# A convolution, attention and expert kernel: the last part in one periodic list, and reciprocal roots moved from POOL to ACT

## The chip, the cores and the metric

The kernel runs on one core of a Trainium2 chip. The core's engines work side by side: TensorE (PE, matmuls; its weight loads are told apart as PEld), VectorE (DVE), ScalarE (ACT), GpSimd (POOL) and SyncE (SP, which here issues transfers). The metric is the time of one execution on the device, in microseconds. The tensors are float32 throughout.

## The reference

The input `x` is 32 images of 128 channels of 64 x 64 pixels. Cut to what matters:

```python
# layer 0: group norm, then a convolution in a learned transform domain, and a residual
x_f = tensor_product(gn(x), k11, k12)             # 64x64 complex matrices along h and w
w_f = tensor_product(weight, kd1, kd2) * 64
prod = einsum('bihw,oihw->bohw', x_f, w_f)         # mixes the 128 channels at each frequency
x = x + real(tensor_product(prod, k21, k22))
# layer 1: tokens are pixels, t is (32, 4096, 128)
n = ln(t)                                         # mean and variance over 128 channels, eps 1e-5
k, v = n @ Wk.T + bk, n @ Wv.T + bv
probs = softmax(einsum('sbe,sbf->sef', k, v) / sqrt(32))   # a 128x128 matrix for each image s
t = t + einsum('sef,sbf->sbe', probs, n)
n = ln(t)
gate = top 2 of softmax(n @ router_w + router_b) over 8 experts, renormalised
t = t + sum over the two chosen experts of gate * (n @ expert_w + expert_b)
```

In the attention the kernel works image by image: for one image it needs the 128 x 128 matrix of products summed over that image's 4096 tokens. Both `ln` steps divide by sqrt(variance + eps), a value for each token.

## The kernel before

The kernel has three parts. The first normalises the images and transforms them into frequencies; the second mixes channels; both are untouched. The last part, from line 788 on, does everything else: the inverse transforms, the residual, attention and experts. It loops over the 32 images, and each image passes through four steps, whose functions are nested in the kernel:

- `transfers(b)`: SP loads eight row tiles `r0` to `r7` (512 KB each, in two transfers) and the image itself, `x` (2 MB, tile `y` in the profile).
- `conv(b)`: for each row tile PE makes the inverse along w, `w0` to `w7` (tile `pu`, L903, into the single PSUM buffer `cv`), and ACT writes it out in two halves, `wo` (L913). Four inverses along h follow, `h0` to `h3` (tile `py`, L925), and DVE adds each to the image, `ho` (L933). The first two images use smaller pieces in the experts' PSUM buffers (L946, L965).
- `front(b)`: PE turns the image into tokens, four token tiles at a time, `pt` (L1049), ACT copies them out, `to` (L1054), DVE takes statistics, `sa` (L1021). DVE makes variances, `va` (L1031 to L1036); POOL raises them to the power -1/2, `pwa` (L1041); DVE makes the shifts, `na` (L1078). ACT normalises, `xg` (L1089), PE sums products, `pg` (L1100). A short chain over the 128 x 128 matrix follows: `gs`, `pb`, `t1`, `pb2`, `sm`, `pr`, `sr`, `sn`, `pc`, `prx`. Then eleven groups of PE products `pp` (L1173), ACT scaling `at` (L1186), DVE addition with statistics `ad` (L1201). The second norm follows: `vb`, `pwb` (again L1041), router logits `lg`, `nb`, `l2`, and the choice of two experts, `f1` to `f5` and `gt` (L1246 to L1276).
- `experts(b)`: ACT normalises, `xn` (L1301), PE turns back, `px` (L1311), ACT copies, `xT` (L1317). For each of 32 token tiles PE makes two halves of expert products, `pe0_0` to `pe31_1` (L1324), and DVE multiplies each by the gates, `m` (L1335). POOL sums the products of two token tiles, `s0` to `s15` (L1360 to L1363). PE turns the result, `st` (tile `po`, L1370), ACT copies it, `so` (L1376), SP stores it (L1377). For the last image five of the sixteen sums are made on DVE instead (L1347).

Buffers: three PSUM tiles for expert products (`pe`), three for everything else of small size (`tl`), two product tiles `tm` between DVE and POOL, two each of `xn`, `xT`, `so`.

Each step is an operation in a plan with its engine, an assumed duration, a due time, what it comes after, and counted buffers that it takes and frees. Due times are the image's number plus an offset, plus a shift for its kind (`SHIFT`), in slots of 114 us. `Plan.run` plays the plan with the assumed durations; at each free engine it starts the earliest due operation that is ready and has its buffers. The order so found is the order of the program: each engine carries out its own instructions in that order and waits where the next one is not ready. The store's transfer is issued in the same operation as ACT's copy `so`.

The table of the power's exponents, `mhalf`, holds -0.5 in 32 columns; variances lie as 128 x 32.

Of the kernel before, what the change touches and what calls it, by code (L numbers as in the profile page):

```python
# [10 lines left out]
F32 = mybir.dt.float32  # L11
# [5 lines left out]
P = 128  # L17
# [7 lines left out]
class Plan:  # L25
# [12 lines left out]
    def run(self):  # L38
# [46 lines left out]
        self.length = now  # L85
        for i in order:
            ops[i][3]()
# [3 lines left out]
def kernel(  # L91
# [737 lines left out]
    def prepare():  # L829
# [23 lines left out]
    plan = Plan({"cv": 1, "pe": 3, "tl": 3, "r": 10, "x": 2, "xg": NG, "xn": 2, "xT": 2, "tm": 2, "so": 2, "gate": 2})  # L853
    SLOT = 114.0

    SHIFT = {
        "ad": -0.15, "at": -0.25, "f": 0.71, "gs": -1.97, "gt": 0.71, "h": -0.24, "ho": -3.5, "kvp": 3.43,
        "kvq": -0.45, "l": 0.71, "lg": 3.61, "m": -0.32, "na": -1.87, "nb": -0.81, "pb": -1.97, "pc": -1.97,
        "pe": 0.16, "pg": -0.08, "pp": 0.19, "pr": -1.97, "prx": -1.97, "pt": -0.23, "pwa": -1.87, "pwb": 3.61,
        "px": 0.15, "r": -0.04, "s": 0.08, "sa": 1.29, "sm": -1.97, "sn": -1.97, "so": 2.13, "sr": -1.97,  # L860
        "st": 1.1, "t": -1.97, "to": 0.06, "va": -1.87, "vb": 3.61, "w": 0.28, "x": -0.68, "xT": -0.68,
        "xg": 0.21, "xn": 2.42,
    }
    made = {}

    def add(b, key, engine, us, at, run, after=(), take=(), free=(), late=0.0):


        names = [k if isinstance(k, tuple) else (b, k) for k in after]
        at += SHIFT.get(key.rstrip("0123456789_"), 0.0)  # L870
        made[b, key] = plan.add(
            engine, us, SLOT * at, run, [made[k] for k in names if k[0] >= 0], take, free, late
        )


    def transfers(b):
# [4 lines left out]
        def load_r(e):  # L881
            def run():
                i = 8 * b + e
                ring, tag = (rp, "r") if i % 10 < 8 else (rp2, "r2")
# [10 lines left out]
        add(b, "x", "SP", 0.1, b + 0.2, load_x if b else (lambda: None), take=("x",), late=12.0 if b else 0.0)  # L895

    def conv(b):
        def w_inverse(e):

            def run():  # L900
                ps = tile_of["cv", b, e] = cps.tile([P, 8, P], F32, tag="cv", name=f"pu{b}_{e}")
                for k in range(8):
# [3 lines left out]
                    )  # L906
            return run
# [31 lines left out]
        def w_inverse_piece(e, oh):  # L939

            def run():
                ps = tile_of["cw", b, e, oh] = eps.tile([P, 8, n], F32, tag="pe", name=f"pw{b}_{e}_{oh}")
                for k in range(8):
                    lo = (2 * k + oh) * n
                    for r in range(2):
                        nc.tensor.matmul(  # L946
                            ps[r * n : (r + 1) * n, k, :], rs[b, e][:, lo : lo + n], qw[:, r, :], start=True, stop=True
                        )
            return run
# [28 lines left out]
        if b < 2:  # L978
            for e in range(8):
                at = b + 0.08 * e  # L980
                for oh in range(2):
                    add(
                        b, f"w{e}_{oh}", "PE", 0.95, at + 0.04 * oh, w_inverse_piece(e, oh),
                        [f"r{e}"] + [(b - 1, f"h{k}") for k in range(4)], ("pe",), ("r",) if oh else (),
# [13 lines left out]
            if b == 0:  # L998
                add(b, "prep", "PE", 3.5, 0.98, prepare, ["h3"], ("pe",), ("pe",))
# [14 lines left out]
    def front(b):  # L1014
# [24 lines left out]
        def power(which):  # L1039
            total, var, nmr, rstd = v[which]  # L1040
            nc.gpsimd.tensor_tensor(rstd, var, mhalf, ALU.pow)  # L1041
# [26 lines left out]
        for g in range(8):  # L1068
# [3 lines left out]
            add(b, f"sa{g}", "DVE", 0.85, at, stats1(g), [f"to{g}"] + (["sa0"] if g else []))  # L1072
        add(b, "va", "DVE", 1.7, s1 + 0.14, lambda: moments(1), [f"sa{g}" for g in range(8)])
        add(b, "pwa", "POOL", 5.5, s1 + 0.14, lambda: power(1), ["va"])

        def nmr1():
            total, var, nmr, rstd = v[1]
# [3 lines left out]
        add(b, "na", "DVE", 0.9, s1 + 0.14, nmr1, ["pwa"])  # L1081
# [74 lines left out]
        add(b, "pb", "PE", 0.35, at, kv1, ["gs"], ("tl",))  # L1156
# [48 lines left out]
        for j, lo in enumerate(range(0, NT, 3)):  # L1205
            m = min(3, NT - lo)
            at = s1 + 0.45 + 0.016 * j
            add(b, f"pp{lo}", "PE", 0.26 * m, at, product(lo, m), ["prx", (b - 1, "lg")], ("tl",), ("x",) if lo == 30 else ())
# [29 lines left out]
        def nmr2():  # L1238
            total, var, nmr, rstd = v[2]
# [41 lines left out]
        add(b, "pwb", "POOL", 5.5, at, lambda: power(2), ["vb"])  # L1281
        add(b, "lg", "DVE", 1.95, at, logits1, ["vb"])
        add(b, "nb", "DVE", 2.1, at + 0.1, nmr2, ["pwb", "lg"])
        add(b, "l2", "DVE", 1.95, at + 0.1, logits2, ["nb"], ("gate",))
# [7 lines left out]
    def experts(b):  # L1292
# [79 lines left out]

        def store(g):
            def run():
                so = wp.tile([P, 512], F32, tag="so", name=f"so{b}_{g}")
                nc.scalar.copy(so, tile_of.pop(("po", b, g)))  # L1376
# [92 lines left out]
```

## Time and profile before

| | |
|---|---|
| median of 3 runs | 6039.6 us (6039.03 to 6046.36) |
| the profiled execution | 6034.45 us, its span 6032.7 us |
| busy PE, PEld, DVE, ACT, POOL | 5884.8, 4672.1, 4220.6, 3757.1, 4205.9 us |
| last part | 2536.5 us to the end |
| granted PE clock, mean | 0.994 |

A line of a profile names the engine, the line of the kernel, and the tiles written and read (`out<-in`). Busy time is the union of an engine's instructions. "Idle before" is the time in which the engine did nothing just before the instruction, with the one that ended it behind `<-`. The chain of waits is followed back from the last instruction, at each step to what released it. PE instructions are pipelined, so that one begins before the last has ended: what a piece costs PE is read from the starts of two that follow each other.

### The profile page before, as it was taken

To read this page: it belongs to the slowest core of one execution; us is meant where nothing else is said; L and a number is where in the kernel's file an instruction comes from. 1 tells how busy PE (TensorE), PEld (TensorE's weight loads), DVE (VectorE), ACT (ScalarE), POOL (GpSimd) and SP (SyncE) were. 2 spreads that over 40 slices of the span, in tenths; PEclk is the share of its full clock that TensorE was granted. 3 is DMA by queue.
4 is the path that set the end of the run, shared out by engine and by line. 5 is a ranking of instruction groups with operands and counts; after the bars stand their busy time and mean duration, and the time that the engine had idled before them with its cause. 6 is when DMAs were issued, how large, how long until landed. Compare 5 with 4: busy or idle time off the path is not lost.

```text
span 6032.7 us, 219314 instructions
## 1 busy us (share of the span) xinstructions
PE 5884.8 (98%) x95372; PEld 4672.1 (77%) x95372; DVE 4220.6 (70%) x7696; ACT 3757.1 (62%) x7057; POOL 4205.9 (70%) x3793
## 2 busy tenths in 40 slices
PE   7999999999999999989999999999999999999998
PEld 7999999999999999866666666666666666666654
DVE  5565545555555555458778787887878788787888
ACT  7666664555555555467766676676767666676663
POOL 2110006666666666538898998989899888998988
PEclk9999999999999999999999999999999999999999
DMA  5767766666666666632222122221322222132100
GB/s 198 240 226 236 236 217 192 174 172 173 171 173 173 171 173 172 171 102 88 81 71 98 57 98 71 83 86 57 106 63 91 78 74 95 57 100 70 66 27 28
DMA packets 554068, 756.74 MB, mean 125 GB/s; under 512 B 58320, under 2 KB 318928, under 8 KB 549008
## 3 DMA queue, kind: packets, MB, share of 16 engines
q1 hardware_dynamic: 550496, 733.64, 40.3%
q8 instruction: 749, 12.27, 0.9%
q0 software_dynamic: 2608, 9.06, 0.5%
q14 instruction: 215, 1.76, 0.1%
HBM read 406.79 MB, written 335.54 MB: 123 GB/s over the span
## 4 chain that ended last, share of the span: by engine, by line
PE 88%; ACT 7%; issue 2%; DVE 1%; POOL 1%; DMA 1%; SPq 0%; POOLq 0%; ACTq 0%; DVEq 0%
PE pe L1324 28%; PE m L658 17%; PE g L636 9%; PE pf L418 7%; PE pu L903 6%; PE pp L1173 4%; PE py L925 4%; PE pg L1100 4%; PE pv L396 3%; PE px L1311 2%; ACT xn L1301 2%; ACT u L913 2%; PE pz L373 1%; ACT z L383 1%; PE pt L1049 1%
## 5 line engine op out<-in xcount | busy, mean ns | idle before, releaser
L1324 PE MATMUL pe<-ew_sb,xT 128*128 128x512 f32 x4096 | 1946.1, 597 | 19.4 <-DVE tm L1335 16.0
L1335 DVE TENSOR_TENSOR tm<-pe,oh 128x512 f32<-128x512 f32 x2028 | 1346.4, 684 | 479.3 <-PE pe L1324 455.5
L1360 POOL TENSOR_TENSOR tm<-tm 128x512 f32<-128x512 f32 x1014 | 1286.1, 1284 | 201.1 <-DVE tm L1335 182.7
L1324 PEld LDWEIGHTS pe<-ew_sb,xT 128*128 128x128 f32 x4096 | 700.9, 191 | 522.9 <-issue 396.1
L647 DVE COPY f<-g 128x1024 f32<-128x1024 f32 x508 | 622.2, 1225 | 648.9 <-PE g L636 648.9
L658 PE MATMUL m<-f,s 128*64 128x64 f32 x32768 | 1070.1, 224 | 1.9 <-issue 1.1
L658 PEld LDWEIGHTS m<-f,s 128*64 128x64 f32 x32768 | 1000.0, 138 | 63.2 <-issue 2.6
L604 POOL COPY s<-l 128x512 f32<-128x512 f32 x512 | 546.0, 1099 | 524.9 <-issue 508.3
L647 ACT COPY f<-g 128x1024 f32<-128x1024 f32 x508 | 514.5, 1013 | 561.0 <-PE g L636 534.8
L1363 POOL TENSOR_TENSOR tk<-tk,tm 128x256 f32<-128x256 f32 x1014 | 753.6, 743 | 79.5
L1361 POOL TENSOR_TENSOR tm<-tm 128x512 f32<-128x512 f32 x507 | 650.4, 1283 | 39.8
L913 ACT COPY u<-pu 64x512 f32<-64x512 f32 x960 | 556.6, 580 | 135.1 <-PE pu L903 121.5
L636 PE MATMUL g<-c,wst 9*128 9x128 f32 x16256 | 599.9, 283 | 3.6 <-issue 3.3
L636 PEld LDWEIGHTS g<-c,wst 9*128 9x128 f32 x16256 | 502.8, 186 | 38.5 <-issue 3.9
L349 POOL TENSOR_TENSOR grstd<-gms,mhalf 128x1 f32<-128x1 f32 x32 | 17.8, 555 | 735.8 <-DVE gms L345 735.8
L1186 ACT ACTIVATE pp<-pp,m 128x128 f32<-128x128 f32 x1024 | 440.9, 431 | 124.1 <-PE pp L1173 99.3
L606 POOL TENSOR_SCALAR s<-l 128x512 f32<-128x512 f32 x256 | 509.5, 1990 | 0.0
L903 PEld LDWEIGHTS pu<-qw,r 128*128 128x128 f32 x3840 | 455.7, 193 | 63.3 <-ACT u L913 49.5
L903 PE MATMUL pu<-qw,r 128*128 128x128 f32 x3840 | 476.3, 278 | 25.6 <-ACT u L913 25.6
L1317 ACT COPY xT<-px 128x512 f32<-128x512 f32 x256 | 150.2, 587 | 560.5 <-PE px L1311 557.5
L418 PE MATMUL pf<-ph,v 128*128 128x128 f32 x4096 | 491.0, 278 | 5.0 <-ACT z L383 1.1
L418 PEld LDWEIGHTS pf<-ph,v 128*128 128x128 f32 x4096 | 466.9, 192 | 14.7 <-ACT z L383 7.1
(177 smaller groups left out, 8573.0 us busy)
## 6 DMA issues: line engine op xcount, KB each, us to landing
xf<-f SPq DMA_DIRECT2D x512, 256.0 KB
pf<-o SPq DMA_DIRECT2D x1016, 128.0 KB
l<-xf SPq DMA_DIRECT2D x1012, 128.0 KB
r<-pf SPq DMA_DIRECT2D x496, 256.0 KB
x<-in_x_dram SPq DMA_DIRECT2D x256, 256.0 KB
out_dram<-so SPq DMA_DIRECT2D x256, 256.0 KB
y<-in_x_dram SPq DMA_DIRECT2D x31, 2048.0 KB
r<-pf POOLq DMA_DIRECT2D x16, 248.0 KB, 7.7
```

The source lines that it names most:

```text
L418: nc.tensor.matmul(pl[:, j * P : (j + 1) * P], vs[b][:, 8 * g + j, :], ph.rearrange("h r m -> h (r m)"), start=True, stop=True,)
L604: nc.gpsimd.tensor_copy(dst, src)
L636: nc.tensor.matmul(pg[g // 2][:, g % 2, m * P : (m + 1) * P], wst[rows, 16 * half + 4 * t + m, :], c[rows].rearrange("r h k -> r (h k)"), ...
L647: copy(f.rearrange("i m (g o) -> i m g o", g=2), tile_of["g", w, half, t][k].rearrange("i g (o m) -> i m g o", o=4))
L658: nc.tensor.matmul(ps[hh * n : (hh + 1) * n, q, :], s[:, h].rearrange("i k b -> i (k b)")[:, B * r : B * r + n], f[:, h, r, :], start=(r = ...
L903: nc.tensor.matmul(ps[:, k, :], rs[b, e][:, k * P : (k + 1) * P], qw.rearrange("w r m -> w (r m)"), start=True, stop=True,)
L913: nc.scalar.copy(u[r * n : (r + 1) * n, :, oh * n + 8 * e : oh * n + 8 * e + 8], ps[oh * n : (oh + 1) * n, :, r * n : (r + 1) * n].rearran ...
L1324: nc.tensor.matmul(ps, tile_of["xT", b, i // 4][:, i % 4, :], ew_sb[:, es, :].rearrange("d e c -> d (e c)"), start=True, stop=True,)
L1335: nc.vector.tensor_tensor(tile_of["tm", b, i // 2][:, i % 2, es, :], tile_of.pop(("pe", b, i, half)).rearrange("p (e c) -> p e c", c=P), t ...
L1360: nc.gpsimd.tensor_tensor(tm[:, k, 0:4, :], tm[:, k, 0:4, :], tm[:, k, 4:8, :], ALU.add)
L1361: nc.gpsimd.tensor_tensor(tm[:, :, 0:2, :], tm[:, :, 0:2, :], tm[:, :, 2:4, :], ALU.add)
L1363: nc.gpsimd.tensor_tensor(t[:, lo : lo + 2, :], t[:, lo : lo + 2, :], tm[:, :, m, :], ALU.add)
```

## The change

The order of the last part is no longer found by playing the plan. A list, `ORDER`, names each step of one period with a stage number. A step of image b stands at b + stage + its position in the list (as a share of the list), plus, for the first two and the last two images, a small offset for its kind (`EDGE`). All steps are sorted by this number, and `Plan.follow` emits them in that order; it asserts that each step stands behind what it needs and that the counted buffers suffice. `SHIFT` goes.

Loads and stores are entries of the list too: `r`, `x`, and `os`, the store, which is split from ACT's copy `so`. A row tile is loaded into whichever of the ten buffers was freed first (`rings`). The counted buffers `x`, `xT` and `gate` are replaced by dependencies on the steps that read them last. The one-off `prep` (three small products and corrections of weights) moves from behind the first image's `h3` to behind its first statistics.

The power -1/2 leaves POOL: ACT takes the logarithm and then the exponential of -1/2 of it, and DVE corrects the result with one Newton step of three operations, ahead of the shifts in `na` and `nb`.

```diff
             ops[i][3]()
 
+    def follow(self, order):
+        ops, room, done = self.ops, dict(self.room), set()
+        for i in order:
+            for k in ops[i][5]:
+                room[k] -= 1
+            assert done.issuperset(ops[i][4]) and min(room.values()) >= 0, i
+            for k in ops[i][6]:
+                room[k] += 1
+            done.add(i)
+        assert len(done) == len(ops) == len(order)
+        for i in order:
+            ops[i][3]()
+
...
-    plan = Plan({"cv": 1, "pe": 3, "tl": 3, "r": 10, "x": 2, "xg": NG, "xn": 2, "xT": 2, "tm": 2, "so": 2, "gate": 2})
+    plan = Plan({"cv": 1, "pe": 3, "tl": 3, "r": 10, "xg": NG, "xn": 2, "tm": 2, "so": 2})
     SLOT = 114.0
...
     made = {}
+    rings, ring_of = [(rp2, "r2")] * 2, {(0, e): (rp, "r") for e in range(8)}
...
-        at += SHIFT.get(key.rstrip("0123456789_"), 0.0)
...
-                i = 8 * b + e
-                ring, tag = (rp, "r") if i % 10 < 8 else (rp2, "r2")
+                ring_of[b, e] = ring, tag = rings.pop(0)
...
-        add(b, "x", "SP", 0.1, b + 0.2, load_x if b else (lambda: None), take=("x",), late=12.0 if b else 0.0)
+        add(b, "x", "SP", 0.1, b + 0.2, load_x if b else (lambda: None), [(b - 2, f"pp{lo}") for lo in range(0, NT, 3)], late=12.0 if b else 0.0)
...
+                rings.append(ring_of[b, e])
...
-                        [f"r{e}"] + [(b - 1, f"h{k}") for k in range(4)], ("pe",), ("r",) if oh else (),
+                        [f"r{e}"] + [(b - 1, f"h{k}") for k in range(4)] + [f"w{e}_0"] * oh,
+                        ("pe",), ("r",) if oh else (),
...
-            if b == 0:
-                add(b, "prep", "PE", 3.5, 0.98, prepare, ["h3"], ("pe",), ("pe",))
...
         def power(which):
             total, var, nmr, rstd = v[which]
-            nc.gpsimd.tensor_tensor(rstd, var, mhalf, ALU.pow)
+            nc.scalar.activation(rstd, var, AF.Ln)
+            nc.scalar.activation(rstd, rstd, AF.Exp, scale=-0.5)
+
+        def newton(which):
+
+            total, var, nmr, rstd = v[which]
+            nc.vector.scalar_tensor_tensor(var, var, -0.5, rstd, ALU.mult, ALU.mult)
+            nc.vector.tensor_tensor(var, var, rstd, ALU.mult)
+            nc.vector.scalar_tensor_tensor(rstd, var, 1.5, rstd, ALU.add, ALU.mult)
 
         def turn(g):
...
+        if b == 0:
+            add(b, "prep", "PE", 3.5, 1.2, prepare, [f"sa{g}" for g in range(8)], ("pe",), ("pe",))
         add(b, "va", "DVE", 1.7, s1 + 0.14, lambda: moments(1), [f"sa{g}" for g in range(8)])
-        add(b, "pwa", "POOL", 5.5, s1 + 0.14, lambda: power(1), ["va"])
+        add(b, "pwa", "ACT", 0.55, s1 + 0.14, lambda: power(1), ["va"])
 
...
         def nmr1():
+            newton(1)
             total, var, nmr, rstd = v[1]
             nc.vector.scalar_tensor_tensor(nmr, total, -0.5, rstd, ALU.mult, ALU.mult)
             nc.vector.tensor_scalar_add(v["above"], nmr, 1.0)
 
-        add(b, "na", "DVE", 0.9, s1 + 0.14, nmr1, ["pwa"])
+        add(b, "na", "DVE", 1.4, s1 + 0.14, nmr1, ["pwa"])
 
...
-        add(b, "pb", "PE", 0.35, at, kv1, ["gs"], ("tl",))
+        add(b, "pb", "PE", 0.35, at, kv1, ["gs"] + ["prep"] * (b == 0), ("tl",))
...
-            add(b, f"pp{lo}", "PE", 0.26 * m, at, product(lo, m), ["prx", (b - 1, "lg")], ("tl",), ("x",) if lo == 30 else ())
+            add(b, f"pp{lo}", "PE", 0.26 * m, at, product(lo, m), ["prx", (b - 1, "lg")], ("tl",))
...
-        add(b, "pwb", "POOL", 5.5, at, lambda: power(2), ["vb"])
-        add(b, "lg", "DVE", 1.95, at, logits1, ["vb"])
-        add(b, "nb", "DVE", 2.1, at + 0.1, nmr2, ["pwb", "lg"])
-        add(b, "l2", "DVE", 1.95, at + 0.1, logits2, ["nb"], ("gate",))
+        add(b, "pwb", "ACT", 0.55, at, lambda: power(2), ["vb"])
+        add(b, "lg", "DVE", 1.95, at, logits1, ["vb"] + ["prep"] * (b == 0))
+        add(b, "nb", "DVE", 2.6, at + 0.1, nmr2, ["pwb", "lg"])
+        add(b, "l2", "DVE", 1.95, at + 0.1, logits2, ["nb"] + [(b - 2, f"m{i}_{h}") for i in range(NT) for h in range(2)])
...
+        def evicted(g):
+            def run():
+                so = tile_of["so", b, g] = wp.tile([P, 512], F32, tag="so", name=f"so{b}_{g}")
+                nc.scalar.copy(so, tile_of.pop(("po", b, g)))
+            return run
+
         def store(g):
             def run():
-                so = wp.tile([P, 512], F32, tag="so", name=f"so{b}_{g}")
-                nc.scalar.copy(so, tile_of.pop(("po", b, g)))
-                nc.sync.dma_start(ov[b][:, g * 512 : (g + 1) * 512], so)
+                nc.sync.dma_start(ov[b][:, g * 512 : (g + 1) * 512], tile_of.pop(("so", b, g)))
             return run
 
...
+            last = [(b - (g < 2), f"pe{4 * ((g - 2) % 8) + k}_{half}") for k in range(4) for half in range(2)]
             add(b, f"xn{g}", "ACT", 1.65, at - 0.1, normal(g), ["nb"], ("xn",))
-            add(b, f"px{g}", "PE", 0.48, at - 0.05, turn(g), [f"xn{g}"], ("tl", "xT"), ("xn",))
-            add(b, f"xT{g}", "ACT", 0.55, at - 0.05, turned(g), [f"px{g}"], (), ("tl",))
+            add(b, f"px{g}", "PE", 0.48, at - 0.05, turn(g), [f"xn{g}"], ("tl",), ("xn",))
+            add(b, f"xT{g}", "ACT", 0.55, at - 0.05, turned(g), [f"px{g}"] + last, (), ("tl",))
             for k in range(4):
...
-                        b, f"pe{i}_{half}", "PE", 0.86, at + 0.125 * (2 * k + half) / 8, expert(i, half), [f"xT{g}"],
-                        ("pe",), ("xT",) if k == 3 and half else (),
+                        b, f"pe{i}_{half}", "PE", 0.86, at + 0.125 * (2 * k + half) / 8, expert(i, half),
...
-            add(b, f"so{g}", "ACT", 0.55, at + 0.25, store(g), [f"st{g}"], (), ("tl",))
+            add(b, f"so{g}", "ACT", 0.55, at + 0.25, evicted(g), [f"st{g}"], ("so",), ("tl",))
+            add(b, f"os{g}", "SP", 0.2, at + 0.25, store(g), [f"so{g}"], (), ("so",), 4.0)
 
...
-    plan.run()
+    ORDER = """
+        s7:4 os2:4 pc:3 pe17_1:4 pe16_0:4 prx:3 ho3:2 r2:0 m16_0:4 pp0:3 pe17_0:4 at0:3 r0:0 pe16_1:4 m17_1:4
+        m17_0:4 pp6:3 m16_1:4 pe18_0:4 at6:3 ad0:3 s8:4 r4:1 pp12:3 m18_0:4 pe19_1:4 at12:3 ad6:3 pe18_1:4 m19_1:4
+        pp9:3 ad12:3 pe19_0:4 at9:3 st3:4 m19_0:4 pe22_0:4 m18_1:4 r1:1 r5:1 so3:4 pp3:3 ad9:3 s9:4 pe23_1:4 at3:3
+        m22_0:4 pp24:3 m23_1:4 pe22_1:4 at24:3 ad3:3 pp21:3 m22_1:4 pe23_0:4 at21:3 ad24:3 pp30:3 pe21_0:4 m23_0:4
+        at30:3 ad21:3 s11:4 pe20_0:4 pp15:3 ad30:3 pe20_1:4 at15:3 m20_0:4 px6:4 pp27:3 m21_0:4 m20_1:4 xT6:4 ad15:3
+        pe21_1:4 at27:3 pp18:3 m21_1:4 pe26_0:4 at18:3 s10:4 ad27:3 pe27_0:4 m26_0:4 xn7:4 pt1:2 m27_0:4 w0:1 ad18:3
+        to1:2 vb:3 pe26_1:4 r3:0 wo0_0:1 pe27_1:4 m26_1:4 wo0_1:1 px7:4 m27_1:4 pe24_0:4 pwb:3 lg:3 s13:4 pt0:2
+        pe24_1:4 m24_0:4 pe25_1:4 st4:4 m24_1:4 so4:4 xT7:4 w1:1 m25_1:4 nb:3 to0:2 pe25_0:4 r6:0 os3:4 wo1_0:1
+        pt2:2 m25_0:4 wo1_1:1 pe30_0:4 l2:3 s12:4 pt3:2 m30_0:4 xn0:3 pe31_1:4 os4:4 w2:1 m31_1:4 to3:2 f1:3 to2:2
+        wo2_0:1 f2:3 wo2_1:1 st5:4 pe30_1:4 pe28_0:4 px0:3 xn3:3 pe31_0:4 m30_1:4 m28_0:4 m31_0:4 w3:1 so5:4 xT0:3
+        f3:3 s15:4 pt5:2 wo3_0:1 st6:4 pe29_0:4 f4:3 wo3_1:1 pe29_1:4 pt4:2 to5:2 so6:4 pe28_1:4 m29_0:4 m29_1:4
+        w4:1 m28_1:4 to4:2 xn1:3 x:1 r7:0 s14:4 f5:3 px3:3 gt:3 wo4_0:1 pt6:2 px1:3 wo4_1:1 pe1_0:3 pe0_0:3 xT1:3
+        xn2:3 pe0_1:3 m0_0:3 m1_0:3 w5:1 m0_1:3 to6:2 px2:3 wo5_0:1 pe1_1:3 wo5_1:1 pe2_0:3 m1_1:3 sa0:2 pe3_1:3
+        s0:3 xn4:3 m2_0:3 pe2_1:3 m3_1:3 os5:4 w6:1 m2_1:3 sa3:2 sa4:2 st7:4 wo6_0:1 pe3_0:3 sa5:2 so7:4 pe4_0:3
+        m3_0:3 wo6_1:1 os7:4 sa2:2 pe4_1:3 s1:3 sa6:2 xT2:3 pt7:2 pe5_1:3 m4_0:3 to7:2 w7:1 m5_1:3 sa1:2 m4_1:3
+        pe5_0:3 wo7_0:1 px4:3 m5_0:3 wo7_1:1 pe7_0:3 sa7:2 s2:3 pe6_0:3 va:2 pe7_1:3 m6_0:3 pwa:2 h0:1 m7_1:3 m7_0:3
+        pe6_1:3 ho0:1 st0:3 xT3:3 m6_1:3 pe8_0:3 na:2 s3:3 pe9_0:3 m8_0:3 xg0:2 h1:1 m9_0:3 xg1:2 pe8_1:3 xg2:2
+        pe10_1:3 m8_1:3 ho1:1 pe9_1:3 xg3:2 pe11_0:3 m9_1:3 pg0:2 s4:3 xn6:3 so0:3 os0:3 pe10_0:3 pg1:2 m10_0:3
+        xg4:2 m11_0:3 pg2:2 m10_1:3 pe11_1:3 xg6:2 pg3:2 m11_1:3 xg5:2 s5:3 pe12_0:3 m12_0:3 xg7:2 h2:1 pe13_0:3
+        xn5:3 xT4:3 pe13_1:3 pe12_1:3 m12_1:3 pg4:2 m13_0:3 m13_1:3 pg5:2 ho2:1 s6:3 pg6:2 pg7:2 gs:2 st1:3 pe14_0:3
+        pb:2 so1:3 t1:2 m14_0:3 pe15_0:3 st2:3 os1:3 os6:4 pb2:2 pe15_1:3 sm:2 pr:2 sr:2 m15_1:3 px5:3 pe14_1:3 h3:1
+        m14_1:3 m15_0:3 xT5:3 sn:2 so2:3
+    """
+    EDGE = {
+        0: """
+            ad:-0.034845 at:-0.021118 f:-0.014009 gs:-0.021096 gt:-0.010620 h:-0.207180 ho:-0.216824 l:0.012459
+            lg:-0.015455 m:-0.003331 na:-0.032004 nb:0.022831 os:0.004524 pb:-0.018290 pc:-0.013503 pe:-0.008479
+            pg:-0.051105 pp:-0.024740 pr:0.001950 prep:-0.045540 prx:-0.020870 pt:-0.443345 pwa:-0.100196
+            pwb:0.001327 px:0.003673 r:-5.521628 s:0.010053 sa:-0.268075 sm:0.003079 sn:-0.020537 so:-0.006809
+            sr:0.003295 st:-0.012519 t:-0.018600 to:-0.381076 va:-0.118094 vb:-0.025144 w:-0.357349 wo:-0.328931
+            x:-6.262117 xT:-0.001212 xg:-0.025470 xn:0.008258
+        """,
...
+        B - 1: """
+            ad:-0.005499 at:-0.002667 f:0.014335 gs:-0.016877 gt:0.008722 h:0.116208 ho:0.113500 l:-0.020371
...
+    edge = {b: {k: float(s) for k, s in (w.split(":") for w in words.split())} for b, words in EDGE.items()}
+    turns, words = [], [w.split(":") for w in ORDER.split()]
+    for p, (key, stage) in enumerate(words):
+        for b in range(B):
+            keys = [key]
+            if b < 2 and key[0] == "w" and key[1:].isdigit():
+                keys = [key + "_0", key + "_1"]
+            elif b < 2 and key.rstrip("0123456789") in ("h", "ho"):
+                keys = [key + "_0", key]
+            elif b == 0 and key == "va":
+                keys = [key, "prep"]
+            for z, k in enumerate(keys):
+                if (b, k) in made:
+                    at = b + int(stage) + p / len(words) + edge.get(b, {}).get(k.rstrip("0123456789_"), 0.0)
+                    turns.append((at + (1e-5 if k == "prep" else z * 1e-6), made[b, k]))
+    plan.follow(list(dict.fromkeys(i for at, i in sorted(turns))))
```

## The prediction

> **What bounds the kernel now.** I read the page first, then the busy time by stretches, the chain of waits, and the timeline where the chain leaves TensorE (PE). The answer by stretches (columns: length, then busy PE, PEld, DVE, ACT, POOL with instructions, clock, DMA share, GB/s) shows a middle period, the end from the last image's inverse transform on, and the start of the last part:
>
> ```profile
> PE 88%; ACT 7%; issue 2%; DVE 1%; POOL 1%; DMA 1%; SPq 0%; POOLq 0%; ACTq 0%; DVEq 0%
> ...
> 4560.80:4667.20 106.40, 105.05 (x746) 71.83 (x745) 85.46 (x190) 73.05 (x168) 95.27 (x83) 1.00 0.24 80
> 5801.00:6032.70 231.70, 197.29 (x709) 105.78 (x708) 192.31 (x412) 97.41 (x237) 203.89 (x182) 0.95 0.07 28
> 2536.50:2743.50 207.00, 179.55 (x2436) 143.55 (x2431) 107.64 (x293) 125.41 (x285) 83.04 (x80) 0.96 0.42 119
> ```
>
> PE is the bound in the middle; in the end no engine is, DVE and POOL being nearest. The chain of waits (start, length, what) gives period and piece prices:
>
> ```profile
> 4500.95 0.89 PE pg L1100 x8
> 4519.10 0.74 PE pp L1173 x6
> 4520.69 2.02 PE py L925 x64
> 4560.83 1.65 ACT xn L1301 x4
> 4565.26 0.59 ACT u L913
> 4567.94 0.44 PE pt L1049 x4
> 4568.38 3.44 PE pe L1324 x8
> 4572.25 1.79 PE pu L903 x16
> 4667.21 1.65 ACT xn L1301 x4
> ```
>
> The same `xn` returns after 4667.21 - 4560.83 = 106.38 us. One image asks of PE 64 expert pieces at 0.86 (55.0), 8 `pu` at 1.79 (14.3), 4 `py` at 2.02 (8.1), 8 `pg` at 0.89 (7.1), ten `pp` at 0.735 and one at 0.49 (7.8), 24 groups of transposes at 0.44 (10.5), some 0.7 for the attention's small products: **103.5**. So 2.9 us of each period is loss. The timeline shows where (start, length, what, idle before it):
>
> ```profile
> 4564.76 0.60 PE L1049 MATMUL pt<-ident,y 128*128 128x128 f32 x4
> 4565.89 2.05 PE L903 MATMUL pu<-qw,r 128*128 128x128 f32 x16 [0.54 <-ACT u L913]
> 4581.72 0.60 PE L1370 MATMUL po<-ident,tk 128*128 128x128 f32 x4
> 4583.11 0.66 PE L1049 MATMUL pt<-ident,y 128*128 128x128 f32 x4 [0.79 <-ACT tk L1054]
> ```
>
> A group of 0.44 is followed after 1.13 and 1.39: 0.7 and 0.95 lost, both to an ACT eviction queued behind another `xn`; a third such place costs 0.2. Some 0.4 is five hand-overs of 0.1, most behind `py`; the rest is spread thin. In the end the chain also runs twice through the power, which waits in POOL's queue and then takes 5.44:
>
> ```profile
> 5861.01 5.45 POOL m L1041
> 5928.24 5.41 POOL m L1041
> ...
> L1041 POOL TENSOR_TENSOR m<-m,mhalf x64: 5428/5440/5615, 2582.9 to 5928.2; 128x32 f32<-128x32 f32 x64
> L1267 ACT ACTIVATE tops<-tops x32: 229/233/234, 2667.5 to 5949.5; 128x32 f32<-128x32 f32 x32
> ```
>
> **What the Trainium skill says.** "Trainium Kernel Development and Optimization", Performance Expectations: matmul busy time misleads because matmuls are pipelined. The trace agrees: 105.05 us busy where starts account for 103.5; hence I count by starts. "ScalarE: Activation LUTs", What ACT_TABLE_LOAD costs: a switch of function set is about 1.28 us of load and 1.38 of drain, 2.66 in all. The trace has a single load, of 1.28 us; no drain can be told in it. The same page, Table sets: the usual exponential set lacks the logarithm, but one set holds both. Which is loaded at `Ln` no run here shows. "GPSIMD Engine Reference", Specifications: DVE instructions with two SBUF inputs contend with POOL. The trace agrees: L1248 takes 0.42 at 2651.85, with no sum running on POOL, and 1.38 as its median.
>
> **The change, part by part.**
>
> *Roots.* Per image POOL loses two powers: -10.9 of its 95.3. PE doesn't wait for POOL in the middle, so this is worth nothing there. ACT gains four instructions of 128x32, priced by L1267: 0.93; and table loads, between none and four (`Ln` and `Exp` each switching, twice) at 2.66: 10.6. I take four, since nothing in the program asks for the common set. ACT is then at 74 to 85 of the period, under PE either way. DVE gains six 128x32 operations of 0.18 to 0.20 (the neighbours L1034 to L1036): 1.1, or 7 if POOL stretches each to the 1.2 that such rows reach in the end; I take 1.5, 87 in all. What counts is what stands behind a root in ACT's queue. I lay the new list out on PE's durations above, from `pc` at 0 to 103.5, and call that a place.
> - `pwa`: variances done at about 72 (`sa7` after `m5_0`, then `va`); root at 72.5 to 77.8; `na` waits for `m6_1` anyway and ends at 76.5 to 79.2; each `xg` is 1.55. `xg0` at 78 to 81 against `pg0`'s place 82.0, `xg2` at 81 to 84 against 84.6, `xg3` by 85.6 against 86.4, `xg7` by 94 against 95.4. Covered even at the dear end, by 0.5 to 1.
> - `pwb`: `vb` done at 28.4, root at 28.9 to 34.2; behind it `so4` and `xT7`, 0.59 each, so `xT7` at 33.5 to 35.4; `pe30_0`'s place is 35.3. The dear end just meets it. The cover is `pt0`, `pe24_1`, `pe25_1`, `st4`, `w1`, `pe25_0`, `pt2`.
>
> *Order, middle.* The losses above must go. `w` pieces start at least 5.2 apart; the single buffer needs 1.79, two evictions of 0.58 and at most one `xn` (1.65), 4.8 with hand-over. Products `pp` stand 1.5 to 2.2 apart, with three buffers; `pp18` (22.0) needs the add of `pp15` (22.1): 0.1. POOL's sums take 5.41 each, 86.6 of the period, and are ready 5 to 8 apart; a third pair finds its buffer, the closest `m18_0` at 6.5 against 5.9. Late next is DVE's selection: `f1` from 38.9, three gate products, `f3` to 49, three more, `gt` to 55, `m0_0`, `m1_0` to 56.3, where `pe1_1` has place 56.3. I allow 0.6 for this and the other bare spots, and keep the hand-overs (0.4): 103.5 + 1.0 = **104.5**, a gain of 1.9. Periods: (5801 - 2743.5) / 106.38 = 28.7. **Gain 54**; 104.0 gives 68, 105.6 gives 22.
>
> *Transfers.* SP now has the stores as entries of its own, so ACT's order no longer places them; the number of DMAs is unchanged. `x` is issued 23 us of places ahead of `ho0`; POOL's load of that size took 11.5 to land. The nearest row load, `r1`, leads `w1` by 22; POOL's took 7.7. On SP `r3` may wait for a row buffer up to 12 us, with `os3` and `os4` behind it and ACT's `so5` waiting for `os3`: at worst 1 us of ACT, which `w3` (1.79) hides. Nothing.
>
> *Start* (2536.5 to 2743.5). PE is busy 179.6 of 207, and counted by starts loses about 35. The list moves `prep` behind the statistics, fills the first images' statistics with `w` and `h` of the next, but leaves the first image's products alone (ACT 11 x 1.4 = 16 against PE 7.8: 8 lost) and its selection nearly so (27 on DVE and ACT against 17 of listed PE work: 10 lost), with 2 at `pb` and some 5 at the seam. Saved 35 - 25 = **10**; bounds 0 and 20.
>
> *End* (5801 on). The powers on the chain cost 10.9; two roots at 0.46 to 5.8 take their place. POOL has left some 34 sums x 5.41 = 184 where it was busy 203.9 of 231.7. But the list runs the last inverse transform 0.1 period (11 us) later against the experts. **Gain 12**; from a loss of 5 to 25.
>
> Sum: 54 + 10 + 12 = 76 off the profiled execution's 6034.45 (span 6032.7 and 1.75 around it), 5958. The median of the runs shown, 6039.6, stands 5.15 above that execution; carried over, **5963**.
>
> **Rivals.**
> - *The list meets PE's own work* (103.9 per period, 71) and both edges come out well (45): 117 off, 5923. For it: no queue but DVE's selection is late in the walk. Against: three spots have under 0.2 of slack.
> - *Part of the slack is spent.* Fixed lists can't swap when an eviction is late. At 105.6 and 5 from the edges: 22 + 5 = 27 off, 6013. For it: DVE rows stretch threefold beside POOL, and the walk uses medians.
> - *Slower: the table loads.* If both loads of `pwb` wait for the variances and the engine drains at each, and the root also starts 3 us later than I have it (DVE stretched), `xT7` misses `pe30_0` by 3; at `pwa` the `xg`s then miss by 1. Period 103.5 + 0.4 + 0.6 + 4 = 108.5, 2.1 x 28.7 = 60 slower, edges unchanged: 6100. It decides from 2.9 - 1.0 = 1.9 us of added stall per image. For it: `pwb` has no slack at the dear end. Against: a load needs no data, and the first one of the trace ran at 10.4 while its ACTIVATE waited until 20.4.
> - *The roots don't load tables* (one common set): the same middle, since ACT isn't the bound, and some 5 off the end: 5958. I count it with the forecast.
>
> **How the numbers follow.** About 0.2%, 12 us, is what a measurement of this kernel can tell from no change. Forecast 0.54, own range 5940 to 5985; first rival 0.17; second 0.17, of which 0.03 lies within 12 us; slower 0.09; 0.03 for a start or end so much worse that it eats the middle's gain. Faster 0.54 + 0.17 + 0.14 = 0.85 and 0.01 of the last: 0.86; same 0.04; slower 0.10. The range reaches from the first rival to the second: 5920 to 6013.
>
> **What would show it.** Right: equal marks in the chain of waits 104.0 to 105.0 apart; no `[.. <-ACT u]` or `<-ACT tk` of over 0.3 before `pu` or `pt`; POOL near 85 busy per period; 128 or 129 table loads; L1041 on ACT. Wrong: PE waiting for `xT` behind a root or for `xg`, PE idle at `pe1_1` by more than 1, a period above 106.4, or an end from the last `py` longer than 228.

## The result, and the profile after

The changed kernel takes **6125.6 us** (median; 6114.65 to 6130.38), the kernel before 6039.45 on the same chip: 1.0137 times as long, interval 1.0120 to 1.0155. The forecast was 5963 with a range to 6013: wrong in sign.

The profiled execution took 6114.65 us (span 6112.9). The chain of waits, by engine, for all of it:

```profile
PE 80%; DVE 13%; ACT 3%; issue 3%; POOL 1%; DMA 0%; SPq 0%; POOLq 0%; ACTq 0%; DVEq 0%
```

TensorE (PE) held 88% of the chain before and VectorE (DVE) 1%. DVE now has 13%, where ACT had 7. The answer by stretches (length, then busy PE, PEld, DVE, ACT, POOL with instructions, clock, DMA share, GB/s) for a middle period and for the end from the last `py` on:

```profile
4556.40:4665.00 108.60, 105.13 (x745) 71.55 (x744) 93.12 (x195) 78.90 (x175) 84.44 (x81) 1.00 0.26 78
5880.10:6112.90 232.80, 188.40 (x675) 97.53 (x671) 189.81 (x406) 100.12 (x234) 179.01 (x170) 0.96 0.06 24
```

PE's work is the same (105.1 busy against 105.05), POOL has 10.8 less, ACT 5.9 more. DVE has 7.7 more, where I had allowed 1.5 for six new operations. Summed line by line over the 27 periods of the table below, those six take 3.9 per image (1.1 in run 1, where nothing stretches them), and the five rows of the logits `lg` take 5.4 where they took 1.9. I cut each run at three events: the first transform piece of the last part, the third copy `gs` (one per image), and the thirtieth.

| us | before | after | difference |
|---|---|---|---|
| until the last part starts (untouched) | 2536.5 | 2541.1 | +4.6 |
| start, to the third `gs` | 270.4 | 279.8 | +9.4 |
| middle, 27 periods | 2872.1 | 2930.2 | +58.1 |
| one period | 106.37 | 108.52 | +2.15 |
| end, from the thirtieth `gs` | 353.7 | 361.9 | +8.2 |

The first row varies between 2536.5 and 2548.0 over all the profiled executions of this study; it is not the change's. Where the middle's time lies, the timeline of PE shows (start, length, what, idle before it and what ended it), all in that one period:

```profile
4599.31 1.13 PE L1342 MATMUL pe<-ew_sb,xT 128*128 128x512 f32 x2 [1.47 <-DVE tm L1353]
4622.50 2.41 PE L1342 MATMUL pe<-ew_sb,xT 128*128 128x512 f32 x5 [0.66 <-DVE tm L1353]
4640.13 1.12 PE L1342 MATMUL pe<-ew_sb,xT 128*128 128x512 f32 x2 [0.16 <-DVE tm L1353]
4647.66 1.55 PE L1342 MATMUL pe<-ew_sb,xT 128*128 128x512 f32 x3 [1.18 <-DVE tm L1353]
```

The ACT evictions that held PE before (0.54 and 0.79) are gone, as the list meant. In their place PE waits four times for a gate product `m` (tile `tm`) of DVE: behind `w1`, at `pe1_1`, and twice behind `h0`. Counted from start to start these waits are 1.62, 0.82, 0.22 and 1.45, **4.1 us** in all. Ahead of the first one, all engines in one timeline show (same columns; lines between are left out):

```profile
4592.73 2.50 POOL L1378 TENSOR_TENSOR tm<-tm 128x512 f32<-128x512 f32 x2 [1.20 <-DVE tm L1353]
...
4593.97 1.53 DVE L1250 TENSOR_TENSOR lg<-lq,m 128x256 f32<-128x256 f32 x1
...
4595.31 1.33 POOL L1379 TENSOR_TENSOR tm<-tm 128x512 f32<-128x512 f32 x1
...
4595.54 1.38 DVE L1251 TENSOR_TENSOR lg<-lg,lq 128x256 f32<-128x256 f32 x1
...
4596.72 1.66 POOL L1381 TENSOR_TENSOR tk<-tk,tm 128x256 f32<-128x256 f32 x2
4596.85 0.95 DVE L1252 TENSOR_TENSOR eq<-m,rws 128x256 f32<-128x256 f32 x1
...
4597.82 0.83 DVE L1253 TENSOR_TENSOR lg<-lg,eq 128x256 f32<-128x256 f32 x1
4598.58 1.87 DVE L1353 TENSOR_TENSOR tm<-pe,oh 128x512 f32<-128x512 f32 x3
```

Each row of `lg` ends 0.28 after an add of POOL's sum: 4592.73 + 2.50 + 0.28 = 4595.51 for L1250, the add of 1.33 for L1251, one each of the two 0.8 adds for L1252 and L1253. With the shift row in front of them (0.88 for 0.18) they take 5.5 us, from 4593.17 to 4598.65. The gate product at 4598.58, whose PSUM buffer PE needs, stands behind them; it reads only one operand in SBUF and is not stretched (three in 1.87). The other waits have stretched rows in front of them too. Ahead of the last one stand the first Newton step and the shifts `na`, of which these are two; at `pe1_1` the last three rows of the gates take 1.24, 1.37 and 1.38:

```profile
4643.13 1.27 DVE L1054 TENSOR_TENSOR m<-m 128x32 f32<-128x32 f32 x1
4644.43 1.19 DVE L1055 SCALAR_TENSOR_TENSOR m<-m 128x32 f32<-128x32 f32 x1
```

In the kernel before, the rows of `lg`:

```profile
4551.60 5.44 POOL L1041 TENSOR_TENSOR m<-m,mhalf 128x32 f32<-128x32 f32 x1 [0.59 <-DVE m L1036]
...
4553.34 0.42 DVE L1233 TENSOR_TENSOR lg<-lq,m 128x256 f32<-128x256 f32 x1
4553.79 0.43 DVE L1234 TENSOR_TENSOR lg<-lg,lq 128x256 f32<-128x256 f32 x1
```

`lg` ran while POOL was in the power, and it ran at full speed: over all 32 images this first row took 0.411 to 0.418. The change takes that power away, a sum takes its place, and the row's median becomes 1.534. So the theory to test: **the power was not only POOL's load but DVE's shelter**. The rivals are the table loads on ACT, the list itself, and DVE's added operations as such.

### The profile page after: what moved, and what is told of

Read it like the earlier page. It is cut to its first block, busy times and chain, and to the rows that moved or that the text cites. A ratio compares the mean times of both kernels' runs of the same rounds, so it can differ in the third digit from the quotient of the medians.

```text
span 6112.9 us, 219433 instructions
## 1 busy us (share of the span) xinstructions
PE 5891.6 (96%) x95372; PEld 4663.3 (76%) x95372; DVE 4447.1 (73%) x7888; ACT 3943.2 (65%) x7313; POOL 3864.5 (63%) x3729
## 4 chain that ended last, share of the span: by engine, by line
PE 80%; DVE 13%; ACT 3%; issue 3%; POOL 1%; DMA 0%; SPq 0%; POOLq 0%; ACTq 0%; DVEq 0%
PE pe L1342 23%; PE m L671 17%; PE g L649 9%; PE pf L431 6%; PE pu L907 5%; DVE tm L1353 5%; PE pg L1117 4%; PE pp L1190 3%; PE pv L409 3%; PE py L930 3%; PE po L1388 1%; PE pt L1063 1%; DVE bs L1027 1%; PE pz L386 1%; ACT z L396 1%
## 5 line engine op out<-in xcount | busy, mean ns | idle before, releaser
L1342 PE MATMUL pe<-ew_sb,xT 128*128 128x512 f32 x4096 | 2000.8, 600 | 133.1 <-DVE tm L1353 127.1
L1353 DVE TENSOR_TENSOR tm<-pe,oh 128x512 f32<-128x512 f32 x2028 | 1312.3, 682 | 330.4 <-PE pe L1342 317.1
L1342 PEld LDWEIGHTS pe<-ew_sb,xT 128*128 128x128 f32 x4096 | 681.6, 191 | 566.4 <-issue 262.8
L1106 ACT ACTIVATE xg<-tk,m 128x128 f32<-128x128 f32 x1024 | 401.1, 482 | 162.6 <-DVE m L1096 162.6
```

Of the source, the lines that this page charges most:

```text
L1342: nc.tensor.matmul(ps, tile_of["xT", b, i // 4][:, i % 4, :], ew_sb[:, es, :].rearrange("d e c -> d (e c)"), start=True, stop=True,)
L1353: nc.vector.tensor_tensor(tile_of["tm", b, i // 2][:, i % 2, es, :], tile_of.pop(("pe", b, i, half)).rearrange("p (e c) -> p e c", c=P), t ...
```

## The experiments

All times are medians; each is compared with the kernel before on its own chip (6039.8 to 6045.4).

**1. Sums that don't disturb.** The changed kernel, with the five adds of each sum replaced by one power of 32 columns, 5.4 us long, so that POOL is as busy but the adds are gone. The output lacks the sums.

```diff
-                for k in range(2):
-                    nc.gpsimd.tensor_tensor(tm[:, k, 0:4, :], ...
...
+                nc.gpsimd.tensor_tensor(
+                    t[:, lo : lo + 2, 0:16]..., one..., tm[:, :, 0:8:4, 0:8], ALU.pow)
```

> The changed kernel, with the five additions of each of POOL's sums (5.41 us together) replaced by a single power of 32 columns (5.44 us in the kernel before), which waits for the same four products; the sums are left out of the output. Three theories. Contention: DVE's two-input operations run up to three times as long beside POOL's additions, and the power, which hardly touches SBUF, used to keep POOL off it while the router logits and the shifts were made. It expects L1250 and L1251 back at 0.42 us, DVE's busy time down by over 5 us a period, PE's three long waits (behind w1, px2 and h0) gone, a period of 104 to 105 and a time of 5990 to 6020. Table loads: ACT is held by two loads at each root; it expects no change, period 108 to 109. List: the fixed order itself is bad; no change either.

Measured: **5974.2**, ratio 0.9892 (0.9876 to 0.9909), period 104.32; the period is as contention had it, the time 16 below its range. The rows of `lg` are back at 0.42. A middle period by stretches:

```profile
4486.40:4590.70 104.30, 104.30 (x745) 71.60 (x744) 77.25 (x195) 78.95 (x175) 86.98 (x17) 1.00 0.27 82
```

PE is busy for all of its 104.30 us, POOL is busier than in the changed kernel (86.98 against 84.44), and DVE has 77.25 instead of 93.12 for the same instructions. So not POOL's load but what it executes makes the loss; and the order, with its two roots on ACT, is worth in the middle what the walk said.

**2. No table loads.** `Identity` for the logarithm, so that ACT keeps one table; 128 loads of 1.28 us disappear.

```diff
-            nc.scalar.activation(rstd, var, AF.Ln)
+            nc.scalar.activation(rstd, var, AF.Identity)
```

> The changed kernel with Ln replaced by Identity, so that ACT never changes its table; the roots in the output are wrong by that, instruction count and sizes stay. Contention: the roots were done before DVE came to them (4595.9 against 4600.4 and 4641.3 against 4642.9), so nothing changes: period 108 to 109, within 15 us of the changed kernel. Table loads: two to four microseconds less a period, 6010 to 6065. List: no change.

Measured: **6117.0**, ratio 1.0129 (1.0114 to 1.0144), period 108.55. The interval overlaps the changed kernel's, and its period is 108.52: the loads are not the cause. ACT's timeline in the changed kernel shows one root of an image, with both loads:

```profile
4592.85 1.28 ACT L1047 ACT_TABLE_LOAD   x1
4594.15 0.23 ACT L1047 ACTIVATE m<-m 128x32 f32<-128x32 f32 x1
4594.40 1.28 ACT L1048 ACT_TABLE_LOAD   x1
4595.69 0.23 ACT L1048 ACTIVATE m<-m 128x32 f32<-128x32 f32 x1
```

The root is done at 4595.9; DVE, busy with the stretched `lg`, comes to its Newton step at 4600.37.

**3. The list alone.** The new list, with the power on POOL and no Newton step.

```diff
-            nc.scalar.activation(rstd, var, AF.Ln)
-            nc.scalar.activation(rstd, rstd, AF.Exp, scale=-0.5)
+            nc.gpsimd.tensor_tensor(rstd, var, mhalf, ALU.pow)
...
-            newton(1)
...
-            newton(2)
```

> The changed kernel's list with the roots as before: POOL's power of 5.44 us at the places of pwa and pwb, no Newton step. Contention: the logits run beside the power again, and the shifts are two operations instead of five: waits behind w1 and h0 mostly gone, some given back since POOL has 10.9 us more to do; period 105 to 106.5, 6000 to 6050. Table loads: the same gain, as ACT is free of them. List: period stays at 108 or over, 6115 or more.

Measured: **6181.3**, ratio 1.0234 (1.0219 to 1.0249), period 110.24: a miss for contention, and in the range that the list theory gave. `lg` is sheltered again (0.42 a row) and PE's wait behind `w1` is gone. But the list leaves a root no room for 5.4 us on POOL: PE waits 1.6 at the gates and 2.3 behind `h0`, both for DVE, and ahead of the second one DVE itself waits at `na` for the power:

```profile
4687.21 1.25 DVE L1093 SCALAR_TENSOR_TENSOR m<-m 128x32 f32<-128x32 f32 x1 [2.49 <-POOL m L1047]
```

So this list is bad with the old roots and good where nothing is stretched (run 1): list and roots can't be priced apart from each other.

**4. The roots alone.** The kernel before with its planner, given the new roots and their assumed durations.

```diff
-            nc.gpsimd.tensor_tensor(rstd, var, mhalf, ALU.pow)
+            nc.scalar.activation(rstd, var, AF.Ln)
+            nc.scalar.activation(rstd, rstd, AF.Exp, scale=-0.5)
...
+            newton(1)
...
-        add(b, "pwb", "POOL", 5.5, at, lambda: power(2), ["vb"])
+        add(b, "pwb", "ACT", 0.55, at, lambda: power(2), ["vb"])
...
```

> The kernel before, order by its planner, with the new roots alone (ACT's logarithm and exponential, the Newton step, planned at 0.55, 1.4 and 2.6 us). Contention: DVE gains some 7 us a period of busy time, as in the changed kernel, and PE waits for it: period 107 to 110, 6060 to 6150. Table loads: slower too, but with ACT's evictions as what PE waits for. List: within 0.3% of before, since the roots are hidden.

Measured: **6145.9**, ratio 1.0173 (1.0158 to 1.0189), period 109.67. DVE's timeline, in the same place:

```profile
4622.68 1.53 DVE L1242 TENSOR_TENSOR lg<-lq,m 128x256 f32<-128x256 f32 x1
4624.25 1.37 DVE L1243 TENSOR_TENSOR lg<-lg,lq 128x256 f32<-128x256 f32 x1
```

The same stretch, with another order around it. Time and period are as contention had them, but not DVE's total: all of its instructions together take only 1.4 us more per image than before (97.0 against 95.6, where I expected some 7), yet the period grows by 3.3: what counts is which rows are stretched. The six new operations are not among the stretched ones here: they take 1.1 us an image, while `lg`'s five rows take 4.8. Under the new roots the list is better than the planner, 6126 against 6146.

**5. No Newton steps.** The changed kernel without its six extra DVE operations.

```diff
-            newton(1)
...
-            newton(2)
```

> The changed kernel without its two Newton steps (six small DVE operations per image; the roots are then as exact as logarithm and exponential give them). Theory, DVE stretched beside POOL's sums at the two places where PE has no slack: of the 4.15 us that PE waits per period, the 1.7 behind the first inverse along h go (the three operations ahead of the shifts are gone), the 1.6 behind w1 stay at least in part (lg is stretched as before; the second Newton step stood behind it, in front of the gate products that PE waits for, so up to 1 of it goes too) and the 0.8 at pe1_1 stays: period 106 to 107, 6050 to 6090. Rival, the order itself: six operations cost what they last in total, 4.6 us of DVE, which PE doesn't notice, period 108.3, 6115 to 6130.

Measured: **6051.1**, ratio 1.0019 (1.0012 to 1.0027), period 106.38. PE waits 1.6 behind `w1` as before the edit, 0.34 behind `h0`, and 0.15 at the gates, where I had expected 0.8 to stay. Six operations of 0.18 to 0.20 us are worth 1.2% of the kernel, over 70 us; they stand in rows of three, each needing the one before, between a root and what PE waits for.

**6. The second root back on POOL.**

```diff
+            if which == 2:
+                nc.gpsimd.tensor_tensor(rstd, var, mhalf, ALU.pow)
+                return
...
-            newton(2)
```

> The changed kernel with the second root of each image back on POOL's power (no Newton step there), the first as changed. Theory, shelter: the logits lg stand beside the 5.44 us power again, in which POOL does not slow DVE, so their five rows go back from 5.6 to about 1.9 and the 1.6 us wait of PE behind w1 goes; the 1.7 behind the first inverse along h stays, the 0.8 at pe1_1 may grow by some tenths because POOL's sums come later: period 106.5 to 107.5, 6065 to 6100. Rival, POOL's time is what counts: with 5.44 more on POOL, the sums fall behind and DVE waits for product buffers: period 109 or more, 6130 or more.

Measured: **6140.1**, ratio 1.0164 (1.0147 to 1.0181), period 108.87: a miss, and the time is the rival's. The shelter is there: `lg`'s rows are 0.42 again and the wait behind `w1` is gone. PE's timeline shows the larger of the waits that are left:

```profile
4528.22 3.70 PE L1344 MATMUL pe<-ew_sb,xT 128*128 128x512 f32 x8 [1.42 <-DVE tm L1355]
4553.44 2.84 PE L1344 MATMUL pe<-ew_sb,xT 128*128 128x512 f32 x6 [1.19 <-DVE tm L1355]
```

The wait at the gates has doubled from 0.66 to 1.42. The power alone does not explain that: run 10, which has no power on POOL, shows 1.36 there. But the rival has a part: summed over the middle, the selection's rows ahead of the gates take 11.1 us an image (9.6 in the changed kernel), and DVE waits 0.9 for the power's result and 0.6 for a product buffer that POOL still holds. These two waits are as long as the 1.5 by which the period exceeds run 10's; that they make it was not tested.

**7. Three holds.** The whole changed kernel, with POOL made to wait for DVE where PE waits for DVE: a copy of one column that needs the last row of `lg`, of the gates and of `na`.

```diff
...
+                held = tile_of.get(({13: "h lg", 14: "h gt", 3: "h na"}.get(j), b + 1))
+                if held is not None:
+                    nc.gpsimd.tensor_copy(one[:, 0:1], held)
                 for k in range(2):
                     nc.gpsimd.tensor_tensor(tm[:, k, 0:4, :], tm[:, k, 0:4, :], tm[:, k, 4:8, :], ALU.add)
...
-        ... r7:0 s14:4 f5:3 px3:3 gt:3 wo4_0:1 ...
+        ... r7:0 f5:3 px3:3 gt:3 s14:4 wo4_0:1 ...
```

> The whole changed kernel; in addition POOL is made to wait, by a copy of one column, until lg is done before it starts sum 13 of the image before, until the gates are done before sum 14 (which moves behind gt in the list), and until the shifts na are done before sum 3. Nothing is left out. Theory, contention at the three places: lg back to about 1.9, gt's and na's rows to 0.2 to 0.4, so PE's waits behind w1 (1.6), behind the first inverse along h (1.7) and at pe1_1 (0.8) mostly go; POOL has 17 us of slack per period to wait in: period 104.4 to 105.5, 5990 to 6035, below both kernels. Rival, the holds only move POOL's sums: they then fall on other DVE rows or free the product buffers late, and PE waits there: period 107 to 109, 6080 to 6150.

Measured: **6037.3**, ratio 0.9995 (0.9987 to 1.0004), period 105.79. Some 88 us come back by delaying an engine; the expected period of 104.4 to 105.5 and time of up to 6035 are just missed, with one wait of PE left, behind `h0`:

```profile
4592.99 1.13 PE L1346 MATMUL pe<-ew_sb,xT 128*128 128x512 f32 x2 [1.36 <-DVE tm L1357]
```

DVE's timeline ahead of it shows three of the six rows of the variances `va`, which no hold covers, beside sum 2, whose adds run from 4588.20 on:

```profile
4588.28 1.29 DVE L1039 TENSOR_TENSOR m<-bs 128x32 f32<-128x32 f32 x1
4589.50 1.31 DVE L1040 TENSOR_TENSOR m<-bs 128x32 f32<-128x32 f32 x1
4590.84 1.27 DVE L1042 TENSOR_SCALAR m<-m 128x32 f32<-128x32 f32 x1
```

The other three rows take 0.18 to 0.22: not every row of a chain waits.

**8. Four holds.** A hold for `va` as well. The edit is shown against run 7:

```diff
...
-                held = tile_of.get(({13: "h lg", 14: "h gt", 3: "h na"}.get(j), b + 1))
+                held = tile_of.get(({13: "h lg", 14: "h gt", 2: "h va", 3: "h na"}.get(j), b + 1))
...
-        ... sa7:2 s2:3 pe6_0:3 va:2 pe7_1:3 ...
+        ... sa7:2 va:2 s2:3 pe6_0:3 pe7_1:3 ...
```

For the last image, `va`'s offset in `EDGE` becomes `sa`'s, 0.001766, so that it stays behind `sa7`.

> The three holds as before and a fourth: POOL also waits until the variances va are done before it starts sum 2 (va stands two places earlier in the list for that). Nothing is left out. Theory, contention: the one wait of PE left with three holds, 1.5 us behind the first inverse along h, comes from va's three rows of 1.27 to 1.31 beside sum 2; va falls from 3.9 to about 2 and the wait goes: period 105.8 less 1.0 to 1.5, 104.3 to 104.8, 5990 to 6015. Rival, the wait comes from the order there (a hand-over from the first inverse to the products that DVE can't meet, whatever its rows take): period stays within 0.3 of 105.8, 6030 to 6045.

Measured: **6004.5**, ratio 0.9928 (0.9914 to 0.9941), period 104.41. It computes all that the changed kernel computes and is faster than both kernels. A period by stretches, and POOL's timeline at a hold:

```profile
4493.20:4597.60 104.40, 104.40 (x745) 71.44 (x744) 85.48 (x195) 78.84 (x175) 84.48 (x85) 1.00 0.26 82
```

```profile
4526.80 1.53 POOL L1392 TENSOR_TENSOR tk<-tk,tm 128x256 f32<-128x256 f32 x2
4531.78 0.18 POOL L1387 COPY one<-lg 128x1 f32<-128x1 f32 x1 [3.46 <-DVE lg L1259]
```

The profile shows no idle time of PE in that period. POOL idles 3.46 us before sum 13 so that `lg` runs at 0.42 a row; with some 20 of the period's 104 us free, POOL can afford it.

**9. Four holds and no Newton steps** (the edits of 8 and 5 together).

> The four holds, and the two Newton steps left out (the roots are then as exact as logarithm and exponential give them). Theory, contention: without the six operations nothing of DVE is late at the three places; what is left is what PE itself asks for, as with the quiet sums: period 104.3 to 104.6, 5980 to 6005; so within 10 of the run with four holds. Rival, Newton's own time on DVE costs PE even unstretched: 1 us or more of the period below the run with four holds, over 25 us less.

Measured: **5992.7**, ratio 0.9913 (0.9899 to 0.9926), period 104.32. The Newton steps, worth over 70 us in run 5, are worth 12 here, a little more than the 10 that I allowed, and only 0.09 of the period. In run 8 they still take 3.7 us an image on DVE, stretched for the most part; PE does not wait for it.

**10. One hold, for `lg`** (7 with the table of holds cut to `{13: "h lg"}` and the list unmoved).

> The changed kernel with one hold alone: POOL waits until lg is done before sum 13 of the image before. Nothing is left out. Theory, the waits are separate and add up: the 1.6 us wait behind w1 goes and the other two stay: period 106.8 to 107.2, 6070 to 6085, about half of what three holds gave. Rival, the slack moves through: PE only comes earlier to the gates and waits there longer: period 108 or more, 6105 to 6130.

Measured: **6093.7**, ratio 1.0078 (1.0064 to 1.0092), period 107.40: between the two theories. PE's timeline:

```profile
4615.11 3.70 PE L1346 MATMUL pe<-ew_sb,xT 128*128 128x512 f32 x8 [1.36 <-DVE tm L1357]
4640.27 2.84 PE L1346 MATMUL pe<-ew_sb,xT 128*128 128x512 f32 x6 [1.19 <-DVE tm L1357]
```

The 1.6 behind `w1` is gone, and half of it comes back at the gates, where 0.66 became 1.36: PE now arrives earlier at a DVE that is as late as before. The waits do not simply add up; in the one order tried, the last to be sheltered brings the most (7 to 8: 1.4 of the period for one hold, where this one brings 1.1).

## Why the prediction was wrong

- **PE's own work, 103.5, and a period of 104.5 with hand-overs: right.** It holds where DVE's rows are not stretched at the places where PE needs them: 104.32, 104.41 and 104.32 in runs 1, 8 and 9. The ACT evictions that cost 0.7 and 0.95 are gone. The first rival's 103.9 was reached in no run.
- **The failed step is DVE's term**: "or 7 if POOL stretches each to the 1.2 that such rows reach in the end; I take 1.5, 87 in all", and with it the walk, which has `f1` and `gt` at the durations of before and does not price `lg` at all. Measured: 93.1 busy in the period shown, 3.9 an image for the six new operations and 3.5 more for `lg`'s rows, and 4.1 us of PE waiting for DVE. The upper bound was in the text, but only for the six new operations. The rows that were already there, `lg` above all, were carried over as they were, although the change removes the instruction beside which they had that duration. I had quoted both ends for another row of that size (L1248), 0.42 with no sum running and 1.38 as a median, and did not ask what POOL would be doing at `lg` afterwards.
- **"PE doesn't wait for POOL in the middle, so this is worth nothing there": wrong.** PE doesn't wait for POOL itself, but removing the power cost `lg` its shelter. The sign depends on the order: under the planner the new roots lose 106 us (run 4), under the list they gain some 56 over the old ones (run 3), where DVE waits for the power.
- **The second rival had the right cause and too small a size.** It named DVE's rows beside POOL, and stopped at 105.6; the period is 108.52. It priced lost slack, and not a row of dependent operations that each wait out an add.
- **Table loads: the count was right, the price was the dear end.** There are four per image, 1.28 us each, each ACTIVATE following within 0.03: 5.1 us an image where I had 10.6. A drain of 1.38 as the Trainium skill gives it ("ScalarE: Activation LUTs", What ACT_TABLE_LOAD costs) is not to be seen beside it. ACT's 73.0 became 78.9, and without the loads the time stays: run 2. The slower rival built on them had the right side and the wrong cause, and the one in which the roots load no tables did not come about.
- **Start: 10 gained was forecast, 9.4 was lost**, over the table's somewhat longer stretch. Run 1 loses 4.4 against before (274.9), so 5.0 goes with the adds. Where the other 4.4 comes from stays open: run 4, with the planner, takes 275.2, about as long as run 1 with the list.
- **End: 12 gained was forecast, 0.9 came.** The stretch that was meant, from the last `py` on, takes 232.8 (233.7 before). The 8.2 lost in the table arise ahead of it: from the thirtieth `gs` to the last `py` it is 129 us instead of 120. POOL's busy time from the last `py` on fell from 203.9 to 179.0, close to my 184, so its load did not set that stretch. In the chain of waits there, the power's 4.7% are gone, and DVE's gate products hold 14.8% where they held 6.5. Run 1's end takes 335.8, which is 17.9 under before, so the forecast's size fits a kernel without the adds. The holds do not bring it (361.3 in run 8); how much of run 1's gain is absent stretch, and how much that its sums are one instruction, was not separated.
- **All together.** Run 1 against before: 55.5 + 17.9 - 4.4 = 69 less in the last part, where I had summed to 76. The changed kernel against run 1: 5.0 + 113.6 + 26.1, some 145 more. So the stretch, of which the term taken at "1.5" an image knew next to nothing, was worth twice the gain of everything else. This is its upper end: run 1 also takes away the stretch that the kernel before had (85.45 busy on DVE in a period there, 77.25 in run 1).

What the Trainium skill says of the cause bears on the size too. "GPSIMD Engine Reference", Specifications, names which DVE instructions contend, those with two SBUF inputs among them. "SBUF — State Buffer", SBUF: two separate sides, adds that the port pair is an exclusive lock, held for a whole instruction, while the other engine blocks. The trace agrees for the adds: a stretched DVE row ends just after an add does, whether it needs 0.18 or 0.42 itself (L1054: 1.27; L1250: 1.53). It does not agree for the power, which also reads two SBUF operands and lasts 5.44: there DVE's rows take 0.42. The measurement decides, and this kernel's time hung on it. Why the power spares DVE no run shows; it reads 128 x 32 values of each operand in its 5.44 us, where an add reads 128 x 512 in 1.27.

## What to carry to other kernels

Before an instruction is taken off one engine, list what runs beside it on the others, and ask at which duration those rows will run beside what moves into its place; a median over the whole kernel hides that. Where two engines slow each other, price a chain of small dependent operations, at its dear end, as one instruction of the other engine each, and look for the places where another engine waits for the slowed one. An engine with slack can be made to wait there: four one-column copies per image on POOL turned 1.4% slower into 0.7% faster.

## What the runs showed of the hardware that was not expected

- A DVE operation of 0.18 to 0.42 us with two SBUF inputs takes up to 1.3 or 1.5 beside POOL's 128 x 512 adds (1.27 each) and up to 0.95 beside its 128 x 256 adds (0.74): where it is stretched, it ends 0.04 to 0.28 after one of them. The add itself grows only from 1.27 to about 1.33.
- One with a single tensor input in SBUF can be stretched too (TENSOR_SCALAR, 0.18 to 1.27 in run 7); the gate products, which take one operand from PSUM, keep some 0.68 apiece beside the adds.
- Beside POOL's power, 5.44 us long, the same operations keep 0.42.
- A switch of ACT's table shows as 1.28 us and no more; the logarithm and the exponential, one behind the other, loaded two tables per root.
